# A graph network layer on one core: the columns' list and seven weight loads issued during table A, the weights' products at step 1, two scans of the checks in the ending

## The chip, the cores and the metric

The kernel runs on one core of a Trainium2 chip. TensorE (PE) multiplies matrices, VectorE (DVE) and ScalarE (ACT) work elementwise, GpSimd (POOL) issues the indirect gathers here, and SyncE (SP) issues most transfers. Each engine runs its instructions in the order in which the program gives them, and waits on semaphores for the others. The metric is the device time of one execution in microseconds (us). The median of three runs of the kernel before is 2132.93 us (2130.94 to 2138.86).

## What is computed

There are 12500 nodes with 64 features, 200000 edges sorted by destination with 32 features, and a hidden width of 128. The reference, cut to what matters:

```python
def mlp(x, W1, b1, W2, b2):
    return relu(x @ W1 + b1) @ W2 + b2
...
msg_in = concatenate([x[src], x[dst], edge_attr])            # 64 + 64 + 32
messages = mlp(msg_in, mW1, mb1, mW2, mb2)                   # 128, then 64
aggregated = segment_sum(messages, dst)
update = mlp(concatenate([x, aggregated]), uW1, ub1, uW2, ub2)
return layernorm(x + update)
```

## The kernel before, in words

The first layer of the message network is split by its three inputs. **Table A** holds the product of every node with the first 64 rows of mW1, **table B** that with the next 64 rows and the bias; both lie in HBM. An edge then needs a row of A (gathered by its source), a row of B (its destinations lie in a narrow window, since edges are sorted) and the product of its own 32 features. The message network's second layer is linear behind its ReLU, so hidden rows are summed over the edges of a node first, and its matrix is multiplied into the update's: that is what `weights()` prepares once (the transposed mW2 as w2T, the product w2u, a row of uz, and two matrices with their means taken off).

**Prelude.** A loop over thirteen chunks of table A, k = 0 to 12, calls `chunk_a`: PE's products (L679), a copy by ACT (L689) and one by DVE (L687) into a tile `tb`, and SP's store of the chunk (L691). The tag `tb` has four buffers. Between the chunks stand the zeroing of two x tiles (L670, L672), the first loads of the loop's operands, the loads of x columns that the loop needs (`others`, L660 and L661), chunk 0 of table B, a list of offsets on DVE, and 48 gathers of x rows on POOL, which serve the first eight steps in the place of table A's rows. After the loop `columns_list()` loads two pieces of the source list (L339) into a tile `cols` and DVE turns them into addresses (L342).

**Loop.** A loop of 258 steps follows, each over six tiles of 128 edges. A step has a node part (L433 in the first eight steps, later L443 with rows gathered from table A), the collecting of the step before (counts L503, sums L507), selection matrices for the next group of two steps on DVE (L276 for rows, L284 for the one-hot band), the edge part of the next step (L414), single columns copied by DVE and ACT (`joined` L392, `singly` L384), gathers on POOL, and `rest(s)`, which does what must be done once at some step. `rest(s)` stands between the edge part of step s + 1 and the node part of step s + 1. Every seven steps or so a range of nodes is finished: closed, updated, normalised and stored.

At step BS = 11, `rest` issues seven loads of small weights on ACT's queue and two on SP's, and prepares constants on DVE; at step 13 it calls `weights()` and then `checks()`. The checks find whether any edge lies outside its window (largest and smallest entry of `drc`, 128 x 1563, by the scans L880 and L881), and whether the node ranges fit. PE adds over the partitions (pf, L892), and a flag decides at the very end whether a general path runs; it doesn't run with this input.

**Ending.** The last two steps, their updates and stores are written out by hand. K is the number of node ranges, K - 1 the last.

**What sets the order.** The schedule is by hand: every engine has its instructions in the order in which the code issues them. Semaphores come from the tiles' dependencies. Transfers of SP and ACT count on eight semaphores, DMAHW0 to DMAHW7, that are handed out in turn over both queues; each transfer first waits for the one before it on its semaphore.

## Time and profile before

| | before |
|---|---|
| median of 3 runs | 2132.93 us |
| lowest, highest | 2130.94, 2138.86 us |
| profiled execution | 2131.12 us |
| its span in the profile | 2129.4 us |
| mean granted clock of PE | 0.783 |
| steps in the loop | 258 |

The span is the time from the first to the last instruction of the profiled execution. A page of the profile gives busy time by engine, the course of it in 40 slices, the transfers by queue, and the costliest groups of instructions by line. The trace behind it answers questions by time, engine, line or tile. "Idle before" names the time for which an engine did nothing ahead of an instruction and what released it; "issue" means that nothing in the profile did, and "remote" that the releaser isn't known.

### The profile page before, as it was taken

Reading aid. Unit: us, or ns where it says so; the run is one execution under the profiler, and the core shown is the slowest. Engines: PE = TensorE matmul, PEld = TensorE weight load, DVE = VectorE, ACT = ScalarE, POOL = GpSimd, SP = SyncE. Lnnn points to the kernel's source line nnn. Section 1 sums busy time; section 2 is a strip of 40 time slices with the busy share of each in tenths; the row PEclk is TensorE's granted clock in tenths of the full one; section 3 lists DMA queues with packets and bytes.
Section 4 is the critical chain, followed back from the end, with each engine's and each line's share of the span. In section 5 each row is a group of like instructions: output and inputs, shape, how many; then the busy total and the mean of one; then the engine's idle time right before and its main releaser. Section 6 shows DMA issues by size and latency. Waiting matters only on the chain. (4 is left out here: it accounts for less than half of the span.)

```text
span 2129.4 us, 48279 instructions
## 1 busy us (share of the span) xinstructions
PE 1680.7 (79%) x10746; PEld 1272.8 (60%) x10746; DVE 1177.9 (55%) x8420; ACT 1568.5 (74%) x8066; POOL 1250.2 (59%) x1330
## 2 busy tenths in 40 slices
PE   3577877887787778777877887887888888888887
PEld 3465656665555556555555656665666666666666
DVE  5436565555555555565554555555555555555555
ACT  2296968759869687789686877777776868687773
POOL 6564665666666566665665555655566666666660
PEclk7677787787787777777887777877787788788889
DMA  8723333322222222223222322323232333333331
GB/s 204 192 77 92 89 95 89 96 85 73 80 75 79 75 75 82 76 79 84 77 82 78 89 80 81 89 83 92 85 85 81 92 87 92 88 93 88 90 88 53
DMA packets 207649, 190.05 MB, mean 89 GB/s; under 512 B 57814, under 2 KB 173998, under 8 KB 207358
## 3 DMA queue, kind: packets, MB, share of 16 engines
q1 hardware_dynamic: 163292, 100.05, 16.7%
q0 software_dynamic: 42272, 85.08, 14.5%
q10 hardware_dynamic: 1794, 1.80, 0.4%
q8 instruction: 90, 1.47, 0.3%
q14 instruction: 201, 1.64, 0.3%
HBM read 168.76 MB, written 18.02 MB: 88 GB/s over the span
## 5 line engine op out<-in xcount | busy, mean ns | idle before, releaser
L242 POOL DMA_INDIRECT xg<-tab_a,src_s x1273 | 1201.6, 944 | 807.5 <-issue 267.4
L384 ACT ACTIVATE xc<-xtop,xbot 128x1 f32 x7912 | 1499.0, 280 | 166.8 <-issue 136.7
L392 DVE TENSOR_TENSOR xc<-xtop,xbot 128x1 int32 x7576 | 634.0, 154 | 494.4 <-issue 479.0
L507 PE MATMUL sums<-band,h 128*128 128x96 f32 x3126 | 538.4, 326 | 155.4 <-issue 107.5
L507 PEld LDWEIGHTS sums<-band,h 128*128 128x128 f32 x3126 | 475.5, 232 | 185.3 <-issue 121.2
L443 PE MATMUL pc<-xg,band 128*128 128x256 f32 (+1 forms) x988 | 447.6, 582 | 27.8 <-issue 26.7
L414 PE MATMUL pc<-rhs,l 64*128 64x128 f32 x3126 | 370.6, 356 | 70.3 <-issue 60.6
L414 PEld LDWEIGHTS pc<-rhs,l 64*128 64x128 f32 x3126 | 293.3, 238 | 122.1 <-issue 94.2
L467 DVE TENSOR_SCALAR h<-pc 128x768 f32<-128x768 f32 x247 | 235.1, 952 | 175.7 <-remote 59.4
L443 PEld LDWEIGHTS pc<-xg,band 128*128 128x128 f32 x988 | 214.8, 240 | 141.1 <-issue 97.0
L276 DVE TENSOR_TENSOR l<-l,cps 128x768 f32<-128x768 int32 (+1 forms) x134 | 126.9, 947 | 132.7 <-PE pc L443 38.8
L503 PEld LDWEIGHTS <-one 128*1 128x1 bf16 x1563 | 57.0, 81 | 224.5 <-issue 219.9
L588 ACT ACTIVATE y<-cps 128x256 f32<-128x256 f32 (+1 forms) x36 | 13.7, 379 | 174.8 <-issue 106.2
L503 PE MATMUL cnt<-band,one 128*1 128x32 bf16 x1563 | 90.7, 180 | 55.3 <-issue 54.8
L571 ACT ACTIVATE hTu<-sums,ub_s 128x416 f32<-128x416 f32 (+1 forms) x36 | 21.6, 599 | 127.9 <-remote 47.4
L417 PE MATMUL pc<-band,xc 64*128 64x128 f32 x484 | 77.4, 313 | 8.5 <-issue 6.8
L679 PE MATMUL pb<-band,xtop 64*128 64x128 f32 x208 | 48.2, 396 | 44.8 <-DVE tb L687 29.4
L284 DVE TENSOR_TENSOR band<-cps,drc 128x384 f32<-128x384 f32 x131 | 71.5, 546 | 19.0 <-remote 16.1
L679 PEld LDWEIGHTS pb<-band,xtop 64*128 64x128 f32 x208 | 40.7, 286 | 53.0 <-DVE tb L687 31.2
L417 PEld LDWEIGHTS pc<-band,xc 64*128 64x128 f32 x484 | 63.9, 227 | 9.8 <-issue 9.7
L581 PE MATMUL cps<-u2c,hTu 128*128 128x64 f32 x284 | 54.0, 340 | 14.6 <-issue 14.0
L242 POOL DMA_INDIRECT xg<-in_x,src_s x48 | 47.6, 992 | 24.0 <-issue 12.8
(110 smaller groups left out, 646.1 us busy)
## 6 DMA issues: line engine op xcount, KB each, us to landing
l<-in_dst_row SPq DMA_DIRECT2D x262, 96.0 KB
l<-in_eT SPq DMA_DIRECT2D x262, 96.0 KB
xg<-tab_a,src_s POOLq DMA_INDIRECT x1273
rhs<-tab_b SPq DMA_DIRECT2D x361, 32.0 KB
tab_b<-tb SPq DMA_DIRECT2D x13, 512.0 KB
rhs<-tab_b SPq DMA_DIRECT2D x387, 16.0 KB
tab_a<-tb SPq DMA_DIRECT2D x12, 512.0 KB
out<-y SPq DMA_DIRECT2D x35, 128.0 KB
```

What stands on the lines that cost most here:

```text
L242: ins = nc.gpsimd.indirect_dma_start(out=a[:, i, :] if s < XG else a[:, i // 2, i % 2, :], out_offset=None, in_=A[:, :] if s >= XG else x[ ...
L276: nc.vector.tensor_tensor(l[r], l[r].bitcast(I32), node[r].unsqueeze(2).broadcast_to([r.stop - r.start, SUP // 2, P]), op=ALU.is_equal)
L284: nc.vector.tensor_tensor(s[:, :nt], slot.unsqueeze(1).broadcast_to([P, nt, WIN]), drc[:, g * SUP:g * SUP + nt].unsqueeze(2).broadcast_to( ...
L384: nc.scalar.activation(o[:, e:e + 1], top.bitcast(F32), AF.Identity, bias=bot.bitcast(F32))
L392: nc.vector.tensor_tensor(o[:, e:e + 1].bitcast(I32), top.bitcast(I32), bot.bitcast(I32), op=ALU.bitwise_or)
L414: done = nc.tensor.matmul(pc[:, b, k, :], L[g][q:q + 64, m, :], rhs[g % 2][q:q + 64, w, :], start=k == 0, stop=ends and not copied)
L417: done = nc.tensor.matmul(pc[:, b, k, :], xc[s][q:q + 64], w1a[q:q + 64], start=False, stop=ends)
L443: added = nc.tensor.matmul(pc[:, b, :m], ident, a[:, b, :m], start=False, stop=True)
L467: nc.vector.tensor_scalar(h, pc, 0.0, None, op0=ALU.max)
L503: nc.tensor.matmul(pn8[:, bass.ds(cs[i] - CBASE, 4 * WIN)].bitcast(F32), one, SB[g][:, k0 + i, :, 1], start=False, stop=ends and i == n - 1)
L507: made.append(nc.tensor.matmul(ps8[:, bass.ds(ws[i] - SBASE[u % 2], 4 * WIDE * WIN)].bitcast(F32), h[:, i % 2, i // 2, :], widened(g, k0 + i),
L679: nc.tensor.matmul(pb[:, h, i, :], (xbot if h else xtop)[64 * h:64 * h + 64, (c + HB * h + i) * P:(c + HB * h + i + 1) * P], w[64 * h:64 * ...
```

## The change

- The loads of `cols` are issued at chunk 8 of table A, the list is made at chunk 11. `cols` still uses a buffer of the tag `tb`, now while the chunks need the four of them.
- The seven weight loads on ACT's queue are issued one each at chunks 2 to 8, behind what ACT does for the chunk; the five preparing operations on DVE stand at chunk 1.
- `weights()` is called at step 1 and not at step 13.
- `checks()` is cut up. The node ranges stay at step 13 (`nodes_checked`). The two scans stand in the ending (`largest`, `smallest`), and what follows from them, with pf on PE, behind the last update (`flagged`).

```diff
@@ -330,7 +330,7 @@
             nc.scalar.copy(xt, pt)
             xs[s] = xt
 
-        def columns_list():
+        def columns_asked():
 
             cols = work.tile([P, 2, 2, P], I32, name="cols", tag="tb", bufs=4)
             for r in range(2):
@@ -338,6 +338,12 @@
                 v = src_row[:, ((LEAD + r * P) * SUB + SUB - 2) * P:]
                 nc.sync.dma_start(cols[:n, r].rearrange("k b e -> k (b e)"),
                                   bass.AP(v.tensor, v.offset, [[SUB * P, n], [1, 2 * P]]))
+            return cols
+
+        def columns_list(cols):
+
+            for r in range(2):
+                n = min(P, NSUB - 1 - LEAD - r * P)
                 for b, base in enumerate((XBASE, YBASE)):
                     nc.vector.tensor_scalar(col_a[:n, r, :, b], cols[:n, r, b], 4.0, float(base), op0=ALU.mult, op1=ALU.add)
 
@@ -780,6 +786,9 @@
         for _ in range(2):
             zeros(todo.pop(0), ZEROS, nc.scalar)
         places_made = offsets()
+        weight_loads = {2: (w2, mW2), 3: (u1a, uW1[D:2 * D, :]), 4: (b2c, mb2.rearrange("(f o) -> f o", o=1)),
+                        5: (uz[D:], uW1[0:D, :]), 6: (ux[ONE:ONE + 1], ub2.rearrange("(o f) -> o f", o=1)),
+                        7: (ub1_s, ub1.rearrange("(f o) -> f o", o=1)), 8: (u2, uW2)}
         for k, c in enumerate(range(0, NB, NCH)):
             copied = chunk_a(c)
             for i, u in enumerate(first[:EACH]):
@@ -817,13 +826,25 @@
                 load(g)
                 select(g)
                 counts(g)
+            if k == 1:
+                nc.vector.memset(uz[:D], 0.0)
+                nc.vector.memset(ux[:D], 0.0)
+                nc.vector.memset(eps, EPS)
+                nc.vector.memset(ones, 1.0)
+                nc.vector.tensor_copy(ux[D:], ident[D:, D:])
+            if k in weight_loads:
+                o, i = weight_loads[k]
+                nc.scalar.dma_start(o, i)
+            if k == 8:
+                cols = columns_asked()
+            if k == 11:
+                columns_list(cols)
             if k > 3:
                 for _ in range(OFFS):
                     next(places_made, None)
         assert not todo
         for _ in places_made:
             pass
-        columns_list()
         assert not first
 
         def rest(s):
@@ -838,21 +859,10 @@
             if s == BS:
                 nc.sync.dma_start(wa, wrow.rearrange("o (p c) -> (o p) c", c=NSUP))
                 nc.sync.dma_start(wb, wnext.rearrange("o (p c) -> (o p) c", c=NSUP))
-                nc.scalar.dma_start(w2, mW2)
-                nc.scalar.dma_start(u1a, uW1[D:2 * D, :])
-                nc.scalar.dma_start(b2c, mb2.rearrange("(f o) -> f o", o=1))
-                nc.vector.memset(uz[:D], 0.0)
-                nc.vector.memset(ux[:D], 0.0)
-                nc.vector.memset(eps, EPS)
-                nc.vector.memset(ones, 1.0)
-                nc.vector.tensor_copy(ux[D:], ident[D:, D:])
-                nc.scalar.dma_start(uz[D:], uW1[0:D, :])
-                nc.scalar.dma_start(ux[ONE:ONE + 1], ub2.rearrange("(o f) -> o f", o=1))
-                nc.scalar.dma_start(ub1_s, ub1.rearrange("(f o) -> f o", o=1))
-                nc.scalar.dma_start(u2, uW2)
+            elif s == 1:
+                weights()
             elif s == BS + 2:
-                weights()
-                checks()
+                nodes_checked()
 
         def weights():
 
@@ -872,25 +882,15 @@
                 nc.vector.tensor_scalar(mean, mean, 1.0 / D, None, op0=ALU.mult)
                 nc.vector.tensor_scalar(w, v, mean, None, op0=ALU.subtract)
 
-        def checks():
-
-            mm = work.tile([P, 4], F32, name="mm", bufs=1)
-            r = E - (NT - 1) * P
-
-            nc.vector.tensor_reduce(mm[:, 0:1], drc, AX.X, ALU.max)
-            nc.vector.tensor_reduce(mm[:, 1:2], drc[:, :NT - 1], AX.X, ALU.min)
-            nc.vector.tensor_tensor(mm[:r, 1:2], mm[:r, 1:2], drc[:r, NT - 1:], op=ALU.min)
+        mm = work.tile([P, 4], F32, name="mm", bufs=1)
+        bad = work.tile([1, 1], F32, name="bad", bufs=1)
+
+        def nodes_checked():
 
             back = work.tile([SUP, NSUP], F32, name="back", bufs=1)
             nc.vector.tensor_tensor(back, wb, wa, op=ALU.is_lt)
             nc.vector.memset(mm[:, 2:3], 0.0)
             nc.vector.tensor_reduce(mm[:SUP, 2:3], back, AX.X, ALU.add)
-            nc.vector.tensor_scalar(mm[:, 0:1], mm[:, 0:1], float(WIN - 1), None, op0=ALU.is_gt)
-            nc.vector.tensor_scalar(mm[:, 1:2], mm[:, 1:2], 0.0, None, op0=ALU.is_lt)
-            nc.vector.tensor_reduce(mm[:, 3:4], mm[:, 0:3], AX.X, ALU.add)
-            pf = psum.tile([1, 1], F32, name="pf", tag="pc")
-            nc.tensor.matmul(pf, mm[:, 3:4], ones, start=True, stop=True)
-
             uf = work.tile([1, K + 1], F32, name="uf", bufs=1)
             nc.vector.tensor_copy(uf[:, :K], usup)
             nc.vector.memset(uf[:, K:], float(N))
@@ -899,11 +899,26 @@
             nc.vector.tensor_scalar(gap[:, :K - 1], gap[:, :K - 1], float(UN), None, op0=ALU.is_gt)
             nc.vector.tensor_scalar(gap[:, K - 1:K], gap[:, K - 1:K], float(min(UN, UL)), None, op0=ALU.is_gt)
             nc.vector.tensor_copy(gap[:, K:], past)
-            bad = work.tile([1, 1], F32, name="bad", bufs=1)
             nc.vector.tensor_reduce(bad, gap, AX.X, ALU.add)
+
+        def largest():
+
+            nc.vector.tensor_reduce(mm[:, 0:1], drc, AX.X, ALU.max)
+
+        def smallest():
+
+            nc.vector.tensor_reduce(mm[:, 1:2], drc[:, :NT - 1], AX.X, ALU.min)
+
+        def flagged():
+
+            r = E - (NT - 1) * P
+            nc.vector.tensor_tensor(mm[:r, 1:2], mm[:r, 1:2], drc[:r, NT - 1:], op=ALU.min)
+            nc.vector.tensor_scalar(mm[:, 0:1], mm[:, 0:1], float(WIN - 1), None, op0=ALU.is_gt)
+            nc.vector.tensor_scalar(mm[:, 1:2], mm[:, 1:2], 0.0, None, op0=ALU.is_lt)
+            nc.vector.tensor_reduce(mm[:, 3:4], mm[:, 0:3], AX.X, ALU.add)
+            pf = psum.tile([1, 1], F32, name="pf", tag="pc")
+            nc.tensor.matmul(pf, mm[:, 3:4], ones, start=True, stop=True)
             nc.vector.tensor_tensor(flag_i, pf, bad, op=ALU.add)
-
-
 
         due = {(UPD[u + 1] if u + 1 < K else NSUB) + 1: u for u in range(K)}
 
@@ -994,6 +1009,7 @@
         collect(FINAL - 1)
         close_counts(K - 2)
         close_sums(K - 2)
+        largest()
         residual(K - 3)
         squares(K - 3)
         columns(K - 1)
@@ -1004,6 +1020,7 @@
         activated(K - 2)
         node_part(FINAL + 1)
         norm(K - 3)
+        smallest()
         store(K - 3)
         collect(FINAL)
         carry(K - 1)
@@ -1021,6 +1038,7 @@
         close_sums(K - 1)
         from_nodes(K - 1)
         update(K - 1)
+        flagged()
         activated(K - 1)
         residual(K - 1)
         squares(K - 1)
```

**Table A's stage on SP.** First the rows of before from the store of chunk 6 on: each row is a line, an operation, output and input tile, the shape, and in brackets the semaphores that it waits for.

```order
L691 DMA tab_a<-tb 128x8x128 [waits DMAHW1_49,DVE_49]
L691 DMA tab_a<-tb 128x8x128 [waits DMAHW2_49,DVE_49]
L660 DMA xtop<-in_x1T 64x4x512 [waits DMAHW3_49]
L661 DMA xbot<-in_x1T 64x4x512 [waits DMAHW4_49]
L297 DMA l_81<-in_eT 32x768 [waits DMAHW5_49]
L297 DMA l_81<-in_eT 32x768 [waits DMAHW6_49]
L691 DMA tab_a<-tb 128x8x128 [waits DMAHW7_49,DVE_49]
L691 DMA tab_a<-tb 128x8x128 [waits DMAHW0_49,DVE_49]
L660 DMA xtop<-in_x1T 64x4x512 [waits DMAHW1_49]
L661 DMA xbot<-in_x1T 64x4x512 [waits DMAHW2_49]
```

The same place in the changed kernel, most of whose line numbers are 6 higher:

```order
L697 DMA tab_a<-tb 128x8x128 [waits DMAHW0_49,DVE_49]
L697 DMA tab_a<-tb 128x8x128 [waits DMAHW1_49,DVE_49]
L666 DMA xtop<-in_x1T 64x4x512 [waits DMAHW2_49]
L667 DMA xbot<-in_x1T 64x4x512 [waits DMAHW3_49]
L297 DMA l_81<-in_eT 32x768 [waits DMAHW4_49]
L297 DMA l_81<-in_eT 32x768 [waits DMAHW5_49]
L697 DMA tab_a<-tb 128x8x128 [waits DMAHW6_49,DVE_49]
L339 DMA cols<-in_src_row 128x256 [waits DMAHW7_49]
L339 DMA cols<-in_src_row 124x256 [waits DMAHW0_49]
L697 DMA tab_a<-tb 128x8x128 [waits DMAHW1_49,DVE_49]
```

The loads of `cols` now stand between the stores of chunk 8 and chunk 9. Each transfer waits on a semaphore of another number than before, because ACT's loads take seven turns. The store of chunk 6, the first row, now waits on DMAHW0, whose last user is the load of u2 on ACT; before, it waited on DMAHW1, whose last user was an SP load of group 1's destination rows. In the same way the store of chunk 4 waits for uz, the destination rows of group 1 for ux, and the first x columns of `others` for ub1.

**The same stage on ACT,** before, from the zeroing behind the copy of chunk 7 to that behind chunk 10:

```order
L672 ACTIVATE xtop<-band 64x784
L689 COPY tb<-pb 128x512 [waits DMAHW7_49,DVE_49,PE_49]
L672 ACTIVATE xtop<-band 64x784
L689 COPY tb<-pb 128x512 [waits DMAHW3_49,DVE_49,PE_49]
L672 ACTIVATE xtop<-band 64x784
L689 COPY tb<-pb 128x512 [waits DMAHW1_49,DVE_49,PE_49]
L672 ACTIVATE xtop<-band 64x784
```

and the same stretch in the changed kernel (`ub_s` is ub1, `u_87` is u2):

```order
L678 ACTIVATE xtop<-band 64x784
L837 DMA ub_s<-in_ub 128x1 [waits DMAHW3_49]
L695 COPY tb<-pb 128x512 [waits DMAHW5_49,DVE_49,PE_49]
L678 ACTIVATE xtop<-band 64x784
L837 DMA u_87<-in_uW 128x64 [waits DMAHW0_49]
L695 COPY tb<-pb 128x512 [waits DMAHW0_49,DVE_49,PE_49]
L678 ACTIVATE xtop<-band 64x784
L695 COPY tb<-pb 128x512 [waits DMAHW1_49,DVE_49,PE_49]
L678 ACTIVATE xtop<-band 64x784
```

Each load stands between the zeroing behind one chunk's copy and the next chunk's copy. The copies of chunks 9 to 12 wait for the store of the chunk three before them, and no more four, because `cols` holds one of the buffers.

**PE around the weights' products.** Before, in step 13, from the edge part of step 14 (`pc<-rhs_79,l_81`) to its node part (L443):

```order
L414 MATMUL pc<-rhs_79,l_81 128x128 [waits DMAHW6_49,DMAHW3_49]
L414 MATMUL pc<-rhs_79,l_81 128x128 x3
L417 MATMUL pc<-band,xc 128x128 [waits Activation_49]
L414 MATMUL pc<-rhs_79,l_81 128x128
L417 MATMUL pc<-band,xc 128x128
L860 MATMUL pw<-band,w_83 64x128 [waits DMAHW5_49,DVE_49]
L864 MATMUL pw_4539<-u1a,w2T 128x128 [waits DMAHW6_49,DVE_49]
L867 MATMUL pw_4542<-u1a,b2c 1x128 [waits DMAHW7_49,DVE_49]
L892 MATMUL pf<-ones,mm 1x1 [waits DVE_49]
L443 MATMUL pc<-xg,band 128x256 [waits DMASW6_49,DMASW0_49]
L443 MATMUL pc<-xg,band 128x256 [waits DMASW7_49,DMASW1_49]
```

In the changed kernel, from the edge part of step 2 to its node part (L439):

```order
L420 MATMUL pc<-rhs_79,l_81 128x128 [waits DMAHW2_49,DMAHW4_49,DMAHW0_49,PE_49]
L420 MATMUL pc<-rhs_79,l_81 128x128 [waits DMAHW5_49]
L420 MATMUL pc<-rhs_79,l_81 128x128 x4
L870 MATMUL pw<-band,w_83 64x128 [waits Activation_49]
L874 MATMUL pw_630<-u1a,w2T 128x128 [waits DVE_49]
L877 MATMUL pw_633<-u1a,b2c 1x128 [waits DVE_49]
L439 MATMUL pc<-band,sums_s_73 128x128 [waits Activation_49]
L439 MATMUL pc<-band,sums_s_73 128x128 x5
```

The three products stand in front of the node part of step 2, eleven steps earlier; pf no longer stands here but behind the last update.

**DVE in the ending,** before, from the closing of the range K - 2 to the last node part:

```order
L528 COPY xw_75<-cnt 1x448 [waits PE_49]
L534 COPY sums_s_73<-sums 128x448 [waits PE_49]
L597 TENSOR_REDUCE ss<-y 128x4 [waits Activation_49]
L453 TENSOR_TENSOR h<-xg,pc 128x768 [waits DMASW3_49,DMASW2_49,DMASW4_49,DMASW1_49,DMASW5_49,DMASW0_49,PE_49]
L456 TENSOR_SCALAR h<-h 128x768 [waits DVE_49]
L609 RECIPROCAL rs<-sd 128x4 [waits Activation_49]
L611 TENSOR_TENSOR y<-cps,rs 128x256 [waits DMAHW5_49,DVE_49]
L453 TENSOR_TENSOR h<-xg,pc 128x256 [waits DMASW6_49,DMASW0_49,PE_49]
```

and in the changed kernel:

```order
L534 COPY xw_75<-cnt 1x448 [waits PE_49]
L540 COPY sums_s_73<-sums 128x448 [waits PE_49]
L906 TENSOR_REDUCE mm<-drc 128x1
L603 TENSOR_REDUCE ss<-y 128x4 [waits Activation_49]
L459 TENSOR_TENSOR h<-xg,pc 128x768 [waits DMASW3_49,DMASW2_49,DMASW4_49,DMASW1_49,DMASW5_49,DMASW0_49,PE_49]
L462 TENSOR_SCALAR h<-h 128x768 [waits DVE_49]
L615 RECIPROCAL rs<-sd 128x4 [waits Activation_49]
L617 TENSOR_TENSOR y<-cps,rs 128x256 [waits DMAHW5_49,DVE_49]
L910 TENSOR_REDUCE mm<-drc 128x1
L459 TENSOR_TENSOR h<-xg,pc 128x256 [waits DMASW6_49,DMASW0_49,PE_49]
```

The two scans of `drc` (L906, L910) stand behind the copy of the sums and behind the norm of the range K - 3; the other rows keep their order.

## The prediction

> **What bounds the kernel now.** The page comes first. Its rows give the span and, per engine, busy time, share of the span and instructions.
>
> ```profile
> span 2129.4 us, 48279 instructions
> PE 1680.7 (79%) x10746; PEld 1272.8 (60%) x10746; DVE 1177.9 (55%) x8420; ACT 1568.5 (74%) x8066; POOL 1250.2 (59%) x1330
> ```
>
> PE is the busiest engine, and its matmuls are neither added nor removed here: four small ones change place. So the change is worth what it does to PE's idle time, 2129.4 - 1680.7 = 448.7 us, at three places: steps 11 to 13, the prelude with steps 1 and 2, and the ending. I went to PE's timeline at the first of them (start, duration, engine, line, operation, tiles; in brackets the idle time ahead of it and what ended that), then to DVE's and ACT's for the same stretch.
>
> ```profile
> 183.40 0.49 PE L417 MATMUL pc<-band,xc 64*128 64x128 f32 x4
> 184.93 0.30 PE L860 MATMUL pw<-band,w 128*64 128x128 f32 x1 [1.04 <-DVE xc L392]
> 187.91 0.79 PE L864 MATMUL pw<-u1a,w2T 64*128 64x128 f32 x2 [2.69 <-DVE w2T L862]
> 189.09 0.58 PE L867 MATMUL pw<-u1a,b2c 64*1 64x128 f32 x2 [0.39 <-DVE w2u L865]
> 195.65 0.19 PE L892 MATMUL pf<-ones,mm 128*1 128x1 f32 x2 [5.97 <-DVE mm L890]
> 195.77 2.08 PE L443 MATMUL pc<-xg,band 128*128 128x256 f32 x4
> ...
> 187.58 0.28 DVE L862 COPY w2T<-pw 64x128 f32<-64x128 f32 x1 [1.53 <-remote]
> ...
> 191.12 1.77 DVE L880 TENSOR_REDUCE mm<-drc 128x1 f32<-128x1563 f32 x1
> ...
> 178.65 3.07 ACT L384 ACTIVATE xc<-xtop,xbot 128x1 f32 x16 [16.72 <-DMA u<-in_uW]
> ```
>
> The reader is to see that the four small matmuls stand ahead of step 14's sum of gathered rows (L443) in PE's own order. PE ends L417 at 183.40 + 0.49 = 183.89 and starts L443 at 195.77: 11.88 us in which it does nothing but 0.30 + 0.79 + 0.58 + 0.19 = 1.86 us of matmuls. Its longest wait, 5.97 us, is for the checks on DVE, whose first scan alone takes 1.77 us. ACT stood idle for 16.72 us earlier because of the weight loads in its queue, but no row of PE's in this stretch waits for ACT, so I count nothing for that.
>
> **Steps 11 to 13: what is removed.** All of the 11.88 us goes from this place. What is late next is an instruction page of PE that arrives there. The DMA view counts packets by queue; the first row below is that of 183.5 to 184.5 us, the second that of 212 to 213 us, both with one 16 KB packet on q8. As many rows of PE's timeline follow the second.
>
> ```profile
> q8 instruction: 1, 0.02, 6.1%
> ...
> q8 instruction: 1, 0.02, 6.7%
> ...
> 217.88 0.55 PE L507 MATMUL sums<-band,h 128*128 128x96 f32 x3 [1.02 <-issue]
> ...
> 219.49 0.35 PE L679 MATMUL pb<-band,xbot 64*128 64x128 f32 x1 [0.27 <-issue]
> ...
> 221.74 1.81 PE L414 MATMUL pc<-rhs,l 64*128 64x128 f32 x12 [1.46 <-DVE h L467]
> ```
>
> After the packet of 212 us PE is idle for 1.02 + 0.27 + 1.46 = 2.75 us that I lay to it, two of the three ended by nothing but issue. The packet of 183 us cost nothing visible, since PE waited anyway. Without that cover I let it cost the same 2.75 us: **-11.88 + 2.75 = -9.1 us.** The bounds are -11.9 (it costs nothing) and -6.4 (twice 2.75). The Trainium skill ("Runtime: NRT & Kernel Launch", section "Instruction fetch mechanics") says that crossing such a page is mostly hidden. The rows after 212 us speak against it; by the rule the term would be -11.9, and that is the fourth rival.
>
> **Prelude: the seven weight loads and the columns' loads.** The order shows this part, not the diff. Every DMA of SP or ACT takes the next of eight counters, and waits until the transfer before it on that counter has landed. Before, the counters of the table's stage were passed on among SP's own transfers. Now ACT's weight loads take seven of the turns, and SP's stores wait for them. The table's chunk 4 waits for uz (issued by ACT at chunk 5), the destination rows of group 1 for ux (chunk 6), the x columns that the loop needs (L660) for ub1 (chunk 7), and the store of chunk 6 for u2, which ACT issues only behind its copy of chunk 8. SP runs in order, so all behind that store waits too. ACT's rows of before, then SP's (L691 is the store of a chunk, L339 the columns' loads, L321 the window for step 2), then the first uses on PE and DVE:
>
> ```profile
> 62.33 0.58 ACT L689 COPY tb<-pb 128x512 f32<-128x512 f32 x1 [14.63 <-remote]
> 62.94 0.85 ACT L672 ACTIVATE xtop<-band 64x784 f32<-64x784 f32 x1
> ...
> 72.01 0.37 ACT L689 COPY tb<-pb 128x256 f32<-128x256 f32 x1 [1.27 <-PE pt L329]
> ...
> 49.36 4.30 SPq L691 DMA_DIRECT2D tab_a<-tb  x2
> ...
> 63.66 4.72 SPq L691 DMA_DIRECT2D tab_a<-tb  x2
> ...
> 77.39 1.91 SPq L339 DMA_DIRECT2D cols<-in_src_row  x2
> 80.54 0.78 SPq L321 DMA_DIRECT2D rhs<-tab_b  x1
> ...
> 84.19 1.65 PE L414 MATMUL pc<-rhs,l 64*128 64x128 f32 x12 [4.31 <-issue]
> 85.60 1.52 PE L433 MATMUL pc<-band,sums_s 64*128 64x128 f32 x12
> ...
> 86.56 0.56 DVE L284 TENSOR_TENSOR band<-cps,drc 128x384 f32<-128x384 f32 x1
> ```
>
> Chunk 8's copy stands at 62.33. Chunks 6 and 7 were stored from 49.36 on, 13 us before it; now they come after it. ACT is free of chunk 8 at 62.94 + 0.85 = 63.79 and issues u2. For the time until a transfer lands I take the window for step 2, from its issue to PE's first use of it: 84.19 - 80.54 = 3.65 us, so the store of chunk 6 goes out at 67.4. What then has to be moved is counted from the sizes below (KB of one issue), and its speed from the stretches of ten us (last columns: granted clock, DMA share, GB/s).
>
> ```profile
> tab_a<-tb SPq DMA_DIRECT2D x12, 512.0 KB
> ...
> xtop<-in_x1T SPq DMA_DIRECT2D x4, 512.0 KB
> ...
> l<-in_eT SPq DMA_DIRECT2D x262, 96.0 KB
> ...
> 50.00:60.00 10.00, 3.55 (x30) 2.96 (x28) 8.96 (x18) 0.00 (x0) 7.87 (x8) 0.50 1.10 269
> 60.00:70.00 10.00, 4.05 (x33) 3.76 (x34) 6.63 (x16) 4.32 (x6) 6.07 (x7) 0.50 0.71 174
> 70.00:80.00 10.00, 8.45 (x83) 6.57 (x81) 0.85 (x2) 3.45 (x7) 2.72 (x3) 0.93 1.07 268
> ```
>
> Chunks 6 to 11 and four transfers of x make ten times 512 KB, the edge rows of group 1 twice 96, the columns' loads some 250: 5.7 MB, at 268 GB/s 21.3 us. From 67.4 that ends at 88.7, and with about 2 us for the small transfers behind it the window for step 2 is there at 91 instead of 84.19: +6.8 us. The table's stage can't hide it, for DMA is already full from 70 to 80. But the copy at 62.33 had itself waited 14.63 us in a stretch in which DMA was overfull (1.10); with the x columns queued later that wait may end some 5 us earlier, and then the loss is below 2. So the bounds are 0 and +7, or +9 if chunk 8's copy comes later too; I take **+5**, nearer to the row as it stands. The Trainium skill ("DMA: Bandwidth & Descriptors", section "Anatomy of one DMA — SWDGE (gpsimd) path") says that a DMA's wait is held on the issuing sequencer before dispatch, which is what makes SP stop here and speaks against the change; SP's row at 63.66 agrees, since no later transfer overtakes it. Its fixed cost of about 2 us, stated for GpSimd's path, in place of 3.65 would make this term smaller by 1.6.
>
> **Step 1: the weights' products.** In PE's order they now stand between step 2's edge part (L414) and its node part (L433), which started at 85.60. DVE reaches the first copy when the one-hot band of group 2 (L284) is done, at 86.56 + 0.56 = 87.12. From that copy to the end of pw3 the rows above take 189.09 + 0.58 - 187.58 = 2.09 us. So the node part starts at 89.21, +3.6. Against it, SP no longer issues the columns' loads (1.91 us, L339) ahead of the window and the rows of group 2: -1.9. I take **+1.7**, with bounds of -1.9 (all of the chain lies in waits that PE has anyway) and +3.6.
>
> **Ending.** DVE's rows of before, where the scans go in:
>
> ```profile
> 2109.01 0.60 DVE L534 COPY sums_s<-sums 128x448 f32<-128x448 f32 x1
> 2111.03 0.42 DVE L597 TENSOR_REDUCE ss<-y 128x4 f32<-128x256 f32 x1 [1.41 <-ACT y L588]
> ...
> 2113.14 0.42 DVE L611 TENSOR_TENSOR y<-cps,rs 128x256 f32<-128x256 f32 x1
> 2116.15 0.62 DVE L453 TENSOR_TENSOR h<-xg,pc 128x256 f32<-128x256 f32 x2 [2.59 <-PE pc L414]
> ```
>
> The first scan runs from 2109.61 for 1.77 us, in 1.41 us of idle time: what follows is 0.36 late. The second starts at 2113.56 + 0.36 and ends at 2115.69, before DVE's next operand is there at 2116.15. The four short operations and pf stand on PE's way to the last residual; I take **+0.2** in all, with bounds of 0 and +3.5 (both scans in full). On this cover the term rests: if the x columns or gathers were later there, the scans would still be covered, since the waits named are for ACT and PE.
>
> **Sum.** -9.1 + 5 + 1.7 + 0.2 = -2.2 us. The profiled execution took 2131.12 us (1.7 more than its span), so this gives 2128.9; it lay 1.8 below the median of 2132.93, so as a median **2131 us**.
>
> **The rivals.**
> 1. *The loads' landing is no hindrance.* Chunk 8's copy comes earlier because less is queued, and the prelude loses nothing: -9.1 + 1.7 + 0.2 = -7.2, a median of 2126. For it speaks the overfull DMA of 50 to 60; against it that SP's order puts 2 MB behind u2 whatever the copy's time is. Chance 0.25.
> 2. *The table's stage becomes a chain, and the kernel slower.* The place is the buffer of chunk 12: ACT's copy of it (72.01) now waits until chunk 9 is stored, and the copies of chunks 9 to 11 for chunks 6 to 8. By then 4 x 512 + 2 x 512 + 192 + 250 KB, 3.6 MB or 13.4 us, have gone out from 67.4, so that the copy stands at 81 to 83, 9 to 11 us late, and ACT's node work of steps 0 and 1 stands behind it. It decides from a loss of 7.2 us, the sum of the other terms. At 11 us the median is 2137; with a further wait of the length of the 4.31 us before L414, 2141. Against it: that wait of 4.31 us is slack for steps 0 and 1. Chance 0.25.
> 3. *The change doesn't give back the wait of steps 11 to 13.* DVE's shorter checks stay in step 13, and step 14's gathered rows might not be there 9 us sooner; a third of the gain, -3, would remain: 2137. Against it: L443 starts 0.1 us after pf, so it waited for nothing else then. Chance 0.08.
> 4. *The page that arrives at 183 us is free*: 2.75 us less than the forecast, 2128. Against it speak the rows after 212 us. Chance 0.1.
>
> **How the numbers follow.** The forecast has 0.32. What a measurement of this kernel can tell from no change is about 0.5%, 10.7 us: below 2122 and above 2144. Faster by that much needs rivals 1 and 4 together, or rival 1 with step 1's chain covered (-11.9 + 0.2 or -9.1 - 1.9 + 0.2, 2121 to 2122): 0.18. Slower needs rival 2 beyond its price, with the upper bound of the ending or of step 1: 0.15. The rest, 0.67, lies within. The range goes from 2120 (rivals 1 and 4, bound of step 1 half reached) to 2141 (rival 2 with its wait).
>
> **What would show it.** In the profile of after: PE's gap between L417 and step 14's L443 near 180 us gone, and 2 to 3 us of issue idle in its place; SP's store of chunk 6 behind ACT's chunk 8, at 64 to 68 instead of 49; PE's edge part of step 2 at 86 to 91 instead of 84; its node part some 5 us behind it, with w2T, w2u and the row of uz between; DVE's two scans in the ending with no PE wait on them. The prediction is wrong if the store of chunk 6 goes out before 55, if PE's first loop steps start no later than before, or if PE waits again at step 13 for what the checks held back.

## The result, and the profile after

The changed kernel takes 2128.74 us (median of 20 runs, 2123.37 to 2132.67), the kernel before, run beside it, 2132.12 us (20 runs, 2127.61 to 2138.86). The medians are 3.4 us apart. The ratio of the two sets of runs is 0.9981, with a 95% interval of 0.9973 to 0.9988: 4.0 us faster, 2.6 to 5.8. That lies within half a per cent and within the range. The profiled execution took 2123.37 us, the fastest of the twenty, so its length is worth little by itself; its rows are read place by place. Two more profiles of the same kernel stand beside it below.

The page's first rows after:

```profile
span 2121.6 us, 48273 instructions
PE 1673.7 (79%) x10746; PEld 1271.8 (60%) x10746; DVE 1178.1 (56%) x8420; ACT 1568.7 (74%) x8066; POOL 1250.8 (59%) x1330
```

PE's share is what it was. **Step 13,** PE's timeline of the changed kernel, with the row of the DMA view for 186 to 187 us ahead of it:

```profile
q8 instruction: 1, 0.02, 6.2%
...
184.79 0.49 PE L423 MATMUL pc<-band,xc 64*128 64x128 f32 x4
185.21 1.13 PE L449 MATMUL pc<-xg,band 128*128 128x256 f32 x4
186.27 0.30 PE L509 MATMUL cnt<-band,one 128*1 128x32 bf16 x6
188.48 1.59 PE L513 MATMUL sums<-band,h 128*128 128x96 f32 x12 [1.91 <-issue]
...
195.01 1.65 PE L420 MATMUL pc<-rhs,l 64*128 64x128 f32 x12 [2.60 <-issue]
```

The node part of step 14 (L449) follows L423 at once, where 11.88 us lay between. An instruction page arrives at 186 us, as at 183 before, and PE then waits 1.91 and 2.60 us. Both rows put the wait down to issue. DVE's rows of the same stretch show otherwise (L473 is the ReLU that writes the `h` which L513 reads):

```profile
187.48 0.94 DVE L473 TENSOR_SCALAR h<-pc 128x768 f32<-128x768 f32 x1
...
194.01 0.94 DVE L473 TENSOR_SCALAR h<-pc 128x768 f32<-128x768 f32 x1
```

The two operations end at 188.42 and 194.95 us, and each time PE goes on 0.06 us later. So PE waits here for DVE's ReLU, as the prediction's last row of PE names it at another step of the kernel before (1.46 us, `DVE h L467`), and no wait at this place is left to the page.

**The table's stage,** ACT and SP of the changed kernel (L695 copies a chunk, L697 stores it, L837 loads a weight, L666 loads x columns for the loop, L321 is the window of step 2):

```profile
47.73 0.35 ACTq L837 DMA_DIRECT2D ub_s<-in_ub  x1
...
54.80 0.58 ACT L695 COPY tb<-pb 128x512 f32<-128x512 f32 x1 [5.61 <-PE pb L685]
54.80 0.33 ACTq L837 DMA_DIRECT2D u<-in_uW  x1
...
64.92 0.58 ACT L695 COPY tb<-pb 128x512 f32<-128x512 f32 x1 [8.66 <-DMA tab_a<-tb]
...
78.32 0.37 ACT L695 COPY tb<-pb 128x256 f32<-128x256 f32 x1 [3.43 <-DMA tab_a<-tb]
...
54.31 0.63 SPq L666 DMA_DIRECT2D xtop<-in_x1T  x1
...
60.07 1.21 SPq L697 DMA_DIRECT2D tab_a<-tb  x2
...
83.15 0.76 SPq L321 DMA_DIRECT2D rhs<-tab_b  x1
```

ACT issues ub1 at 47.73, and SP's x columns, which wait for it, go out at 54.31 instead of 43.80 before. ACT issues u2 at 54.80, and the store of chunk 6 goes out at 60.07, where it went at 49.36. ACT's copies of chunk 9 (64.92) and of chunk 12 (78.32) then wait for stores, which no copy's row in the profile of before shows. The stretches of ten us (busy time by engine, then granted clock, DMA share and GB/s) show the hole that this leaves. The first row is that of before, the others are those of the changed kernel:

```profile
40.00:50.00 10.00, 4.66 (x38) 4.08 (x40) 9.33 (x24) 4.32 (x6) 7.56 (x9) 0.50 0.96 259
...
40.00:50.00 10.00, 2.48 (x20) 1.89 (x18) 5.83 (x16) 4.32 (x6) 5.66 (x7) 0.50 0.41 103
50.00:60.00 10.00, 4.15 (x32) 3.56 (x32) 9.40 (x21) 1.44 (x2) 7.79 (x8) 0.50 1.01 252
60.00:70.00 10.00, 5.80 (x39) 4.97 (x39) 8.07 (x18) 2.88 (x4) 8.15 (x7) 0.50 1.08 259
70.00:80.00 10.00, 1.34 (x12) 1.25 (x13) 1.42 (x5) 1.34 (x3) 1.89 (x2) 0.50 1.10 279
```

In the changed kernel DMA is idle for more than half of 40 to 50 us, where its share was 0.96 before; from 50 on it is full.

**Step 1,** PE's rows of the changed kernel:

```profile
87.56 0.94 PE L420 MATMUL pc<-rhs,l 64*128 64x128 f32 x12
88.43 0.30 PE L870 MATMUL pw<-band,w 128*64 128x128 f32 x1
89.84 0.48 PE L874 MATMUL pw<-u1a,w2T 64*128 64x128 f32 x2 [1.11 <-issue]
90.71 0.38 PE L877 MATMUL pw<-u1a,b2c 64*1 64x128 f32 x2 [0.38 <-issue]
91.01 1.45 PE L439 MATMUL pc<-band,sums_s 64*128 64x128 f32 x12
```

Against the profile of before, step 2's edge part (L420) starts 3.4 us later and its node part (L439) 5.4 us later, with the three products between them.

**Ending,** DVE of the changed kernel:

```profile
2101.27 1.76 DVE L906 TENSOR_REDUCE mm<-drc 128x1 f32<-128x1563 f32 x1
2102.95 0.40 DVE L603 TENSOR_REDUCE ss<-y 128x4 f32<-128x256 f32 x1
...
2105.27 1.77 DVE L910 TENSOR_REDUCE mm<-drc 128x1 f32<-128x1562 f32 x1
2107.87 0.62 DVE L459 TENSOR_TENSOR h<-xg,pc 128x256 f32<-128x256 f32 x2 [0.83 <-PE pc L420]
```

Both scans lie in idle time: behind the second one DVE still waits 0.83 us for PE.

### The profile page after: what moved, and what is told of

Read it like the earlier page. It is cut to its first block, busy times and chain, and to the rows that moved or that the text cites. A ratio compares the mean times of both kernels' runs of the same rounds, so it can differ in the third digit from the quotient of the medians.

```text
span 2121.6 us, 48273 instructions
## 1 busy us (share of the span) xinstructions
PE 1673.7 (79%) x10746; PEld 1271.8 (60%) x10746; DVE 1178.1 (56%) x8420; ACT 1568.7 (74%) x8066; POOL 1250.8 (59%) x1330
## 4 chain that ended last, share of the span: by engine, by line
PE 49%; issue 20%; DVE 19%; another core or an unknown queue 6%; DVEq 2%; ACT 1%; DMA 1%; SPq 0%; ACTq 0%; POOL 0%; POOLq 0%
PE sums L513 16%; PE pc L449 12%; DVE xc L398 10%; PE pc L420 10%; DVE h L473 4%; DVE l L276 3%; DVEq L366 2%; PE cps L587 2%; PE cnt L509 2%; PE cps L585 2%; PE sums L572 2%; PE sums L565 1%; PE pc L423 1%; DVE band L284 1%
## 5 line engine op out<-in xcount | busy, mean ns | idle before, releaser
L513 PE MATMUL sums<-band,h 128*128 128x96 f32 x3126 | 533.3, 324 | 166.9 <-issue 104.2
L513 PEld LDWEIGHTS sums<-band,h 128*128 128x128 f32 x3126 | 469.8, 230 | 197.6 <-issue 119.0
L449 PE MATMUL pc<-xg,band 128*128 128x256 f32 (+1 forms) x988 | 446.0, 580 | 34.1 <-issue 33.2
L420 PE MATMUL pc<-rhs,l 64*128 64x128 f32 x3126 | 369.4, 356 | 84.7 <-issue 61.0
L420 PEld LDWEIGHTS pc<-rhs,l 64*128 64x128 f32 x3126 | 292.4, 239 | 134.8 <-issue 89.7
L473 DVE TENSOR_SCALAR h<-pc 128x768 f32<-128x768 f32 x247 | 234.9, 951 | 161.7 <-PE sums L513 67.6
L449 PEld LDWEIGHTS pc<-xg,band 128*128 128x128 f32 x988 | 216.7, 242 | 146.2 <-issue 101.2
L423 PE MATMUL pc<-band,xc 64*128 64x128 f32 x484 | 79.2, 317 | 15.6 <-issue 15.4
L423 PEld LDWEIGHTS pc<-band,xc 64*128 64x128 f32 x484 | 65.7, 230 | 15.9 <-issue 15.8
L585 PE MATMUL cps<-ux,xw 128*128 128x64 f32 x284 | 50.1, 326 | 6.5 <-issue 6.0
```

What stands on the lines that cost most here:

```text
L420: done = nc.tensor.matmul(pc[:, b, k, :], L[g][q:q + 64, m, :], rhs[g % 2][q:q + 64, w, :], start=k == 0, stop=ends and not copied)
L423: done = nc.tensor.matmul(pc[:, b, k, :], xc[s][q:q + 64], w1a[q:q + 64], start=False, stop=ends)
L449: added = nc.tensor.matmul(pc[:, b, :m], ident, a[:, b, :m], start=False, stop=True)
L473: nc.vector.tensor_scalar(h, pc, 0.0, None, op0=ALU.max)
L513: made.append(nc.tensor.matmul(ps8[:, bass.ds(ws[i] - SBASE[u % 2], 4 * WIDE * WIN)].bitcast(F32), h[:, i % 2, i // 2, :], widened(g, k0 + i),
L585: nc.tensor.matmul(py[:, i], xw[u % 2][:, i * P:(i + 1) * P], ux, start=i == 0, stop=False)
```

## The experiments

Twelve runs on three chips, four to a chip. Each was timed beside the kernel before on its own chip, and ratios are to that. The first four ran where the kernel before takes 2158.13 us, the next four where it takes 1682.71 us (of which the last section speaks), the last four where it takes 2133.31 us.

**The theory:** SP's stores wait, through the shared counters, for loads that ACT issues late; that loses 5 us up to step 2, and the gap ahead of step 14 (PE's idle time between L423 and step 14's node part) gives back 9. **The rivals:** the columns' tile or the mere bytes lose the 5 us; the two parts of the gap cover each other, so that only both together help; the gap's end is eaten by the instruction page.

**e1_again and e9_after: the changed kernel again,** on the first and the third chip, no edit.

> The changed kernel once more, to see how far its profile repeats, since the profiled execution (2123.4 us) was the fastest of twenty. Theory (the prelude pays for ACT's loads): the store of chunk 6 at 58 to 66 us, the edge part of step 2 at 87 to 91 (before: 84.2), the gap ahead of step 14's node part gone again, a ratio of 0.997 to 0.999 to the kernel before. Rival (the prelude's loss is chance): the edge part of step 2 within 1 us of 84.2.

> The changed kernel on the chip of this comparison, as the measure for the three beside it. Theory: a ratio of 0.997 to 1.000 to the kernel before, with a loss of 4 to 7 us up to step 2 and a gain of 8 to 11 us ahead of step 14's node part. Rival (the sum of the two depends on chance in the prelude alone): ratio above 1.000.

Measured: 2155.80 us, ratio 0.9988 (0.9976 to 1.0001), and 2129.24 us, ratio 0.9984 (0.9974 to 0.9994). The store of chunk 6 stands at 63.23 and 63.91 us, step 2's edge part at 90.95 and 89.72. So the loss in the prelude is no chance: 3.4, 6.8 and 5.5 us in three profiles, against that of before. A measure on one chip is e11 below, whose prelude is that of the kernel before: it starts step 2 at 83.06 us, 6.7 us ahead of e9 beside it. SP's waits name the cause. In e9 its stores wait 6.3 us for uz and 3.7 us for u2; in the profile of before they wait for DVE and ACT alone.

**e2_sp_loads and e2_again: SP issues the weight loads,** on the first and the second chip.

```diff
-                nc.scalar.dma_start(o, i)
+                nc.sync.dma_start(o, i)
```

> The changed kernel with the seven weight loads issued by SP and not by ACT, at the same chunks: same bytes, same number of turns on the counters, but no store of SP waits any more for something that ACT issues. Theory (SP's stores waited for ACT's loads): the store of chunk 6 back at 49 to 54 us and the edge part of step 2 at 84 to 86, a median 1 to 4 us below the changed kernel's. Rival 1 (the columns' tile, which takes one of four buffers, delays the copies of chunks 9 to 12): chunk 6 at 49 to 54, but step 2 still at 87 or later, median as the changed kernel. Rival 2 (the transfers' number or bytes): chunk 6 still at 58 or later.

> SP issues the seven weight loads, nothing else differs from the changed kernel; for the comparison on this chip. Theory: as in its first run, the store of chunk 6 at 49 to 54 us, the edge part of step 2 at 83 to 86, a ratio of 0.995 to 0.998 to the kernel before. Rival (its first profile was a lucky one): chunk 6 at 58 or later in this one, ratio 0.998 or more.

Measured: 2150.97 us, ratio 0.9967 (0.9956 to 0.9978), and 1679.24 us, ratio 0.9974 (0.9958 to 0.9990). SP's and PE's rows of the first:

```profile
50.16 0.74 SPq L697 DMA_DIRECT2D tab_a<-tb  x1
...
83.55 0.94 PE L420 MATMUL pc<-rhs,l 64*128 64x128 f32 x12
```

The store of chunk 6 is back at 50, and step 2 starts 0.6 us earlier than in the profile of before. The bytes and the number of turns are the same as in the changed kernel, and so is the columns' tile; only the issuer differs. That tells the theory from both rivals, and beside the changed kernel's 2155.80 it is 4.8 us, more than the 1 to 4 expected. (On the second chip chunk 6 was stored at 39.16 and step 2 began at 70.16; its prelude is shorter as a whole, so my times for it did not apply.)

**e3_loads_only: the kernel before, with only the weight loads and the five preparing operations moved,** on the first chip. The edit is the part of the change's diff on `weight_loads` and `k == 1`, and what it takes out of step 11.

> The kernel before with nothing changed but the place of the seven weight loads and the five preparing operations (chunks 1 to 8 of table A). Theory: the store of chunk 6 at 58 to 66 us and the edge part of step 2 at 86 to 90, as in the changed kernel; the 11.9 us gap ahead of step 14's node part stays; median 2 to 5 us above the kernel before. Rival (ACT's 16.7 us of idle time at step 11 was worth something): the loss in the prelude is made up by step 14 and the median is that of before or below.

Measured: 2164.56 us, ratio 1.0031 (1.0019 to 1.0043), 6.4 us slower, more than the 2 to 5 expected. Its rows on SP and PE:

```profile
64.33 1.01 SPq L691 DMA_DIRECT2D tab_a<-tb  x2
...
90.64 0.94 PE L414 MATMUL pc<-rhs,l 64*128 64x128 f32 x12 [2.99 <-issue]
```

The loads alone make the kernel slower, at the place that was named. At step 13 PE waits longer than before; the row of before has 1.04 us there:

```profile
192.76 0.42 PE L860 MATMUL pw<-band,w 128*64 128x128 f32 x1 [3.53 <-DVE xc L392]
```

**e4_weights13: the changed kernel with the products back at step 13,** on the first chip.

```diff
-            elif s == 1:
+            elif s == BS + 2:
                 weights()
-            elif s == BS + 2:
                 nodes_checked()
```

> The changed kernel with the weights' products back at step 13. Theory (each part pays its own PE wait): the node part of step 2 starts 1.5 to 2.5 us after its edge part instead of 3.5; ahead of step 14's node part 4 to 7 us of the 11.9 come back (the products and their waits for DVE, without the scans' 6 us); median 1 to 4 us above the changed kernel's. Rival (the instruction page that arrives there is hidden again by it): the gap costs 4 to 7 us but 3 to 4 us of issue waits behind it go, and the median is within 1.5 us of the changed kernel's.

Measured: 2162.22 us, ratio 1.0017 (1.0008 to 1.0026), 6.4 us above the changed kernel on that chip, more than the 1 to 4 expected. From step 14's edge part to step 15's it takes 16.90 us instead of 12.01 in e1: the products' part of the gap is 4.9 us, in the range named. Step 2's node part starts 0.74 us behind the start of its edge part, less than the 1.5 to 2.5 expected.

**e5_scans13: the changed kernel with the scans, what follows them and pf back at step 13,** on the second chip (`largest`, `smallest` and `flagged` called there and not in the ending).

> The changed kernel with the scans, the operations behind them and pf back at step 13, the weights' products left at step 1. Theory (the gap ahead of step 14's node part was the sum of two waits): PE waits there again for the checks, 5 to 7 us between the edge part's end and the node part; the ending is 0 to 0.5 us shorter; median 3 to 6 us above the changed kernel's. Rival (the scans ran beside work that PE had waited for anyway, the products alone made the gap): less than 2 us of gap, median within 2 us.

Measured: 1687.29 us, ratio 1.0028 (1.0014 to 1.0042). PE waits for the checks again:

```profile
148.78 0.49 PE L423 MATMUL pc<-band,xc 64*128 64x128 f32 x4
157.30 0.19 PE L923 MATMUL pf<-ones,mm 128*1 128x1 f32 x2 [8.03 <-DVE mm L921]
157.42 2.07 PE L449 MATMUL pc<-xg,band 128*128 128x256 f32 x4
```

The gap is 157.42 - 149.27 = 8.15 us, more than the 5 to 7 expected. The changed kernel wasn't run on this chip, so the median can't be set beside it. From step 14's edge part to step 15's it takes 16.34 us, against 8.96 in e2_again on this chip, which has the scans in the ending (and SP as issuer of the loads).

**e7_split and e10_split: SP issues the loads, and the three products stand at steps 1, 2 and 3,** on the second and the third chip.

```diff
...
-            elif s == 1:
-                weights()
+            elif s in (1, 2, 3):
+                weights[s - 1]()
...
```

> SP issues the weight loads as in the run before this, and the three products stand at steps 1, 2 and 3, one in each, so that PE never waits for DVE's copy of the product before. Theory (what step 1 costs is PE's wait for DVE, 1.5 to 3.5 us, and not the 1.2 us of matmuls): the node part of step 2 starts 0.3 to 0.8 us behind its edge part's end; median 1 to 3 us below that of the kernel with SP's loads alone. Rival (that wait lies in PE's next instruction-page stall anyway): within 1 us of it.

> SP issues the weight loads and the three products stand at steps 1, 2 and 3. Theory: a ratio of 0.994 to 0.997 to the kernel before, 4 to 9 us below the changed kernel, of which the loads give 4 to 6 and the split 1 to 3. Rival (the split's wait lies in stalls that PE has anyway in steps 2 and 3): no more than SP's loads alone gave, a ratio of 0.9965 to 0.998.

Measured: 1678.13 us, ratio 0.9975 (0.9960 to 0.9989), and 2126.23 us, ratio 0.9965 (0.9951 to 0.9979). The split does what it says: step 2's node part follows 1.10 us behind the start of its edge part in e10, against 3.62 in e2. But from step 2's edge part to step 4's it takes 22.19 us, against 21.93 in e2 on another chip. On the second chip the two medians are 1678.13 and 1679.24. So the rival holds as far as it was measured: the split is worth nothing that can be told. The version is still 3 us faster than the changed kernel beside it, less than the 4 to 9 expected.

**e8_sp_cols: SP issues the loads, and the columns' list stands behind the table as before,** on the second chip.

```diff
-            if k == 8:
-                cols = columns_asked()
-            if k == 11:
-                columns_list(cols)
...
+        columns_list(columns_asked())
```

> SP issues the weight loads, and the columns' loads and list stand behind the table again, as before the change. Theory (with SP free of ACT's loads the columns' loads cost 1.9 us of SP ahead of step 2's operands): the edge part of step 2 1 to 2 us later than with the columns' loads at chunk 8, median 0 to 2 us above. Rival (the tile of the columns takes a buffer of the copies, and giving it back makes the copies of chunks 9 to 12 earlier): the edge part of step 2 earlier by 1 to 3 us.

Measured: 1680.17 us, ratio 0.9984 (0.9969 to 0.9999). Step 2's edge part starts at 71.33 against 70.16 in e2_again: 1.2 us later, as the theory said. The medians (0.9 us apart, intervals overlapping) don't tell.

**e11_scans_only: the kernel before with only the scans, what follows them and pf in the ending,** on the third chip.

> The kernel before with nothing changed but the scans, the operations behind them and pf, which stand in the ending. Theory (the gap of 11.9 us was 6 us for the checks and 6 for the products): the gap ahead of step 14's node part 5 to 7 us shorter, 2 to 3 us of instruction-page stalls behind it, median 2 to 5 us below the kernel before, no cost in the ending. Rival (the page stall takes it all): within 1.5 us of the kernel before.

Measured: 2128.83 us, ratio 0.9980 (0.9971 to 0.9989). PE's rows:

```profile
183.21 0.49 PE L417 MATMUL pc<-band,xc 64*128 64x128 f32 x4
184.38 0.30 PE L860 MATMUL pw<-band,w 128*64 128x128 f32 x1 [0.68 <-DVE h L467]
185.76 0.48 PE L864 MATMUL pw<-u1a,w2T 64*128 64x128 f32 x2 [1.07 <-DVE band L284]
186.62 0.38 PE L867 MATMUL pw<-u1a,b2c 64*1 64x128 f32 x2 [0.38 <-issue]
186.93 1.13 PE L443 MATMUL pc<-xg,band 128*128 128x256 f32 x4
```

The gap shrinks to 186.93 - 183.70 = 3.23 us, by more than the 5 to 7 expected. The page stalls expected behind it aren't there: the one long wait up to step 15's edge part is 0.97 us, for DVE's ReLU (L467). With nothing else changed the scans alone are worth 4.5 us by the medians, as much as the whole change.

**e12_weights_only: the kernel before with the loads issued by SP during table A and the products at step 1,** checks and columns as before, on the third chip.

> The kernel before with the weight loads issued by SP during table A and the products at step 1; the checks stay whole at step 13 and the columns' loads behind the table. Theory: the gap ahead of step 14's node part 4 to 6 us shorter, the node part of step 2 2 to 4 us later against its edge part, median 1 to 4 us below the kernel before. Rival (the checks' wait covers what the products took): the gap as long as before, median 1 to 3 us above.

Measured: 2126.35 us, ratio 0.9964 (0.9953 to 0.9975): 7 us, more than expected. PE's rows:

```profile
182.63 0.49 PE L417 MATMUL pc<-band,xc 64*128 64x128 f32 x4
191.13 0.19 PE L893 MATMUL pf<-ones,mm 128*1 128x1 f32 x2 [8.01 <-DVE uf L897]
191.41 2.04 PE L443 MATMUL pc<-xg,band 128*128 128x256 f32 x4
```

The gap is 8.29 us: the checks hold PE by themselves, and without the products it is 3.6 us shorter, a little less than the 4 to 6 expected. The two parts neither cover nor need each other.

## Why the prediction came out

The table puts the steps of the prediction beside what the traces show, from single executions on the first and third chip and the two profiles from the start; a column "2 to 4" is the time from the start of step 2's edge part to that of step 4's, in us. e1 to e4 come from the chip where the kernel before takes 2158 us, e9 to e12 from that where it takes 2133 us, so differences between rows of two chips hold a difference of chips too.

```
                   start of 2   2 to 4   11 to 14   14 to 15   257 to the end
before                  84.19    20.50      28.31      20.07      27.07
changed                 87.56    21.52      25.19      11.00      27.30
e1_again                90.95    22.06      25.99      12.01      27.39
e9_after                89.72    21.83      25.38      10.98      27.59
e2_sp_loads             83.55    21.93      26.07      11.04      26.87
e10_split               83.86    22.19      24.68      11.73      26.95
e3_loads_only           90.64    19.91      26.11      22.83      26.82
e4_weights13            90.55    21.60      26.16      16.90      27.55
e11_scans_only          83.06    20.47      28.54      11.69      26.88
e12_weights_only        85.10    20.71      26.29      16.45      26.51
```

- **The gap at steps 11 to 13 (-9.1).** The wait went as forecast: 11.00 - 20.07 = -9.1 in the changed kernel, -9.1 in e9, -8.1 in e1. That 2.75 us of it would come back was right only by luck, for the page isn't what PE waits for. The two waits behind it end 0.05 to 0.06 us after DVE's ReLU (L473) in e1, e2, e9 and e10 too, and in those four the first one begins before the page arrives (in e2 at 184.84, the page at 185.29). The prediction's 2.75 also contained 1.46 us that its own row put down to DVE's ReLU (L467). The Trainium skill says that crossing such a page is mostly hidden ("Runtime: NRT & Kernel Launch", section "Instruction fetch mechanics"). The rows at this place don't speak against it; what the other waits that only issue ends are due to isn't shown.
- **The table's stage (+5).** Right in place and in size: +3.4, +6.8 and +5.5 at step 2's edge part, +6.7 on one chip (e9 against e11), and e2 shows the cause. The working was off in terms that in part cancelled: chunk 8's copy came at 54.80 and not at 62.33, as the first rival had it, and the store of chunk 6 went out at 60.07 to 63.91 and not at 64 to 68. But u2 needed 60.07 - 54.80 = 5.3 us and not 3.65 until the store behind it went out, and the x columns had already been held from 43.80 to 54.31. The 5.3 us goes with the traffic: DMA's share was 0.96 to 1.07 there, and in e3, where it was 0.41 (62 to 64 us), the store followed u2's issue after 64.33 - 62.58 = 1.75 us.
- **Step 1 (+1.7).** The products stand in the rows where they were put: step 2's node part starts 3.45 us behind the start of its edge part, and 1.41 before, so the products cost 2.0 there (2.8 to 3.3 in e9 and e1, where it starts 4.26 and 4.68 behind) where 3.6 was worked out. Over steps 2 to 4 the changed kernel takes 1.0 to 1.6 us more than before; e4, without the products, takes 1.1 more too, so the size is no surer than that.
- **The ending (+0.2).** The scans lie where the rows had room. From step 257 on, runs with them there take 26.87 to 27.59 us, those without 26.51 to 27.07; a cost of some tenths.
- **The sum (-2.2).** The measured -4.0 (2.6 to 5.8) has the right sign and is larger. The term that was mis-sized is that of steps 11 to 13: from step 11 to step 15 the kernel before takes 28.31 + 20.07 = 48.38 us, the changed kernel 36.19, 38.00 and 36.36, which is 10.4 to 12.2 less where 9.1 was counted. That is nearer to the fourth rival's -11.9, whose condition (the page is free) fits the rows above.
- **ACT's idle time at step 11, priced at nothing.** Steps 11 to 14 take 28.31 and 28.54 us in the two kernels whose weight loads stand at step 11, and 24.68 to 26.29 in the eight others: 2.7 us less on average. By itself this is worth nothing at step 15. In e3, which has it without the rest, PE comes to step 14 sooner and then waits 3.53 instead of 1.04 us for DVE, and steps 11 to 15 take 48.94 us against 48.38. In e4 and e11 the products stand at step 13 and the scans in the ending; e4, with its loads in the prelude, takes 43.06 us and e11 40.23 (on another chip). Whether part of it lasts once the products are gone too wasn't tried apart.
- **The slower rival** had its mechanism in the trace (copies of chunks 9 and 12 waiting for stores), but against the profile of before the loss was 3.4 to 6.8 us, under the 7.2 it needed, and the gap gave back more than was counted. e3, without the gap's gain, shows it as a slower kernel.

What stays open: the parts don't add. The scans alone give 4.5 us, loads (by SP) and products alone 7.0, and both together 7.2 in e2 and 7.1 in e10, not 11.5. In the traces both gains are there at step 15, and differences of several us come and go over the 240 steps behind it (e11 is 8.6 us ahead of the profile of before at step 15 and 0.9 behind it at the last step). No run here tells whether something in the loop takes the surplus back or single profiles just differ by that much.

## What to carry to other kernels

Moving a small load to a quieter time is not free where transfers take turns on a few counters: look in the order for who now waits for whom, and let the queue that must not stop issue the load itself. Where PE stands behind several engines' small work in its own order, measure each piece by itself; here the scans alone, and the products alone with their loads issued by SP, were each worth at least as much as the whole change, and the same loads issued by ACT took 5 to 6 us back. And where a wait is put down to issue, look at what the other engines end at that moment before blaming the instruction fetch: here it was DVE's ReLU, 0.06 us earlier.

## What the runs showed of the hardware

The same kernel takes 2133 to 2158 us on some chips and 1683 on another. The page's first rows for e2, on the first chip and then on the second, with the group of the edge part's matmuls from each (busy us, mean ns of one, then idle time before them and what ended it):

```profile
span 2148.5 us, 48239 instructions
PE 1683.4 (78%) x10710; PEld 1289.8 (60%) x10746; DVE 1179.2 (55%) x8420; ACT 1571.2 (73%) x8066; POOL 1250.1 (58%) x1330
L420 PE MATMUL pc<-rhs,l 64*128 64x128 f32 x3126 | 371.4, 358 | 76.4 <-issue 57.3
```

```profile
span 1678.9 us, 48239 instructions
PE 1382.0 (82%) x10710; PEld 1082.9 (65%) x10746; DVE 1161.0 (69%) x8420; ACT 1540.0 (92%) x8066; POOL 1253.9 (75%) x1330
L420 PE MATMUL pc<-rhs,l 64*128 64x128 f32 x3126 | 285.2, 316 | 37.7 <-DVE h L473 27.8
```

DVE, ACT and POOL are busy as long on both, within 2%. On the second chip PE is granted a mean clock of 0.881 instead of 0.774. Most of the idle time ahead of this group is ended by issue on the first chip (57.3 us) and by DVE on the second (27.8 us), and there ACT, not PE, is the busiest engine at 92%. A change tuned against PE's idle time on the one chip meets another bound on the other. That is why each kernel's time was compared with that of the kernel before on the same chip.
